# The causal convolution's taps as diagonal matmuls in the opening of a two-layer hybrid kernel

## The chip, the cores and the metric

The kernel runs on one core of a Trainium2 chip. The metric is the time of one execution on the device in microseconds; several runs are taken and their median is used. All times below come from the runs of the kernel before or from one execution of it that the hardware profiler recorded.

## The reference

The input is x of 8 images with 384 channels and 32×32 pixels, in float32. Layer 0 normalises x over the channels and runs a Mamba block over the 1024 pixels in both directions. Layer 1 is causal attention and a feed-forward block with binarized weights and quantized activations, of which only the first five batches need the feed-forward result. What the change touches is this part of layer 0:

```python
xz = jnp.einsum('blc,ec->ble', x, in_proj_w)
u, z = jnp.split(xz, 2, axis=-1)
uc = jax.lax.conv_general_dilated(u.transpose(0, 2, 1), conv1d_w[:, None, :], (1,),
        [(D_CONV - 1, 0)], ..., feature_group_count=C)      # D_CONV = 4
u = silu((uc + conv1d_b[None, :, None]).transpose(0, 2, 1))
x_dbl = jnp.einsum('blc,ec->ble', u, x_proj_w)
dt, Bm, Cm = jnp.split(x_dbl, [dt_rank, dt_rank + D_STATE], axis=-1)
delta = softplus(jnp.einsum('blr,dr->bld', dt, dt_proj_w) + dt_proj_b)
...
h = dA * h + dBu            # the scan over 1024 steps, 16 states
```

The convolution has four taps and one weight per channel and tap. It is done twice, on the sequence and on the reversed one.

## The kernel before, in words

Channels lie on the 128 partitions, so a batch is three chunks (`c`) of 128 channels × 1024 pixels, and each row of 1024 is handled in two halves (`h`) of 512[...]. Every stage is a function that appends steps to a list; lists are interleaved by estimated durations, and a scheduler then fixes the order of the instructions on each engine ahead of time.[...]

`before_scan(b)` makes what the scan of one batch needs. It loads x into a large buffer and normalises it (L324 to L329). For each chunk it then does:

- `in_proj`: three matmuls a half for `u` and for `z` (L336), copied out of PSUM by ACT (L343). The weights `win` are loaded for each chunk.
- `conv(c, d, h)`: one convolution group. In the loop over four taps, the first (s = 0) is an ACT pass that writes the PSUM bank `acc` (L352), the other three are DVE instructions that add weight × shifted `up` to it (L362). ACT adds the bias and writes `u` to SBUF (L363).
- the SiLU on ACT (L423), the sum of both directions (L427), and stores of `u`, `z` and their sum to DRAM.
- `local`: the 3×3 depthwise convolution of the local branch, nine taps, eight of them on DVE (L383), with its gate (L442 to L452).
- `project`: the matmuls xp (L476), summed on DVE in `xd` (L487).

When the three chunks are done, `xd`'s rows for B and C go to DRAM, and `delta` makes 12 tiles of delta and u × delta: a matmul (L507), four ACT passes (L510 to L513), four DVE instructions (L514 to L517) and two stores (L520).

The scan works in units of two states for one half of one chunk in one direction: 96 units a batch. For each, SP loads B and C rows broadcast over the partitions (`bc`), POOL multiplies u × delta by B (`g`, L564), ACT makes the exponential `da` (L577), DVE runs two scans (L582), POOL multiplies by C (L588), and PE transposes and sums in PSUM (L598, eight instructions). POOL's multiplications are kept in program order, and `g` has seven buffers.

**The opening** is what `run(begin)` and `run(first, beside)` make (L1088 to L1096). `begin` is `before_scan` of the first batch. `first` holds the scan units of that batch, and `beside` what goes on beside them: the rest of the first batch's gates, `before_scan` of the second batch, the binarizing of both feed-forward weights (`binarize`, loads at L205 issued from ACT's queue), and `before_scan` of the third and fourth batch. After that come the scans of the other seven batches beside attention (it starts with the output projection, L667) and feed-forward. In that later part `before_scan` of the remaining four batches is laid between feed-forward steps.

Banks of PSUM: two called `s`, two `pt`, two `da`, one `y`, one `av`. In the opening `before_scan` takes turns on `s` and `pt`. In SBUF there are six large buffers of three chunks × 1024 (`btile`), used for x, for weights, for attention and for feed-forward.

Of the kernel before, what the change touches and what calls it, by code (L numbers as in the profile page):

```python
# [12 lines left out]
ALU = mybir.AluOpType  # L13
# [4 lines left out]
P = 128  # L18
B, C, H, W = 8, 384, 32, 32
L = H * W  # L20
NC = C // P
# [5 lines left out]
DCONV = 4  # L27
# [16 lines left out]
ORDER = (0, 1, 2, 3, 5, 6, 4, 7)  # L44
# [3 lines left out]
V_NORM, V_CW, V_CB, V_DTB, V_D, V_DW, V_DWB, V_BP, V_B2, V_ALOG = 0, 1, 5, 6, 7, 8, 17, 18, 19, 20  # L48
# [4 lines left out]
def kernel(  # L53
# [16 lines left out]
    nc = tc.nc  # L70
# [11 lines left out]
    def ctile(name, shape, dt=F32):  # L82
        return const.tile(shape, dt, name=name, tag=name)

    def btile(name):
        return big.tile([P, NC, L], F32, name=name, tag="big")
# [16 lines left out]
    def half(h):  # L103
        return slice(h * HB, (h + 1) * HB)
# [23 lines left out]
    vec = ctile("vec", [P, NC, NV])  # L128
# [8 lines left out]
    for d in range(2):  # L137
        nc.scalar.dma_start(out=wdt[d * DW : d * DW + RANK, :], in_=w_dt)
        nc.scalar.dma_start(
            out=wdt[d * DW + RANK : d * DW + RANK + 1, :],  # L140
# [13 lines left out]
    ident = ctile("ident", [P, P])  # L154
# [147 lines left out]
                    )  # L302


    def before_scan(b, tags, emit, later=None):

        st = {}
        turns = itertools.cycle(tags)
# [1 line left out]
        def bank_of(name):  # L310
            return bank(name, next(turns))
# [33 lines left out]
        def conv(c, d, h):  # L345

            acc = bank_of(f"u{d}_{b}_{c}_{h}")
            up = st["up", c]
            for s in range(DCONV):
                w = vec[:, c, V_CW + DCONV - 1 - s : V_CW + DCONV - s]  # L350
                if s == 0:
                    nc.scalar.activation(acc, up[:, half(h)], AF.Copy, scale=w)  # L352
                    continue
                lo, hi = h * HB, (h + 1) * HB
                if d == 0:
                    t0, t1 = max(lo, s), hi
                    tap = up[:, t0 - s : t1 - s]
                else:
                    t0, t1 = lo, min(hi, L - s)
                    tap = up[:, t0 + s : t1 + s]  # L360
                to = acc[:, t0 - lo : t1 - lo]
                nc.vector.scalar_tensor_tensor(to, tap, w, to, ALU.mult, ALU.add)  # L362
            nc.scalar.activation(  # L363
                st["u", d, c][:, half(h)], acc, AF.Identity, bias=vec[:, c, V_CB : V_CB + 1]
            )

        def local(c, h):

            acc = bank_of(f"loc_{b}_{c}_{h}")
            r0, rows = h * (HB // W), HB // W  # L370
            img = acc.rearrange("p (i j) -> p i j", j=W)
            src = st["xn"][:, c, :].rearrange("p (i j) -> p i j", j=W)
            nc.scalar.activation(  # L373
                acc, st["xn"][:, c, half(h)], AF.Copy, scale=vec[:, c, V_DW + 4 : V_DW + 5]
            )
            for k in range(9):
                di, dj = k // 3 - 1, k % 3 - 1
                if k == 4:
                    continue
                i0, i1 = max(r0, -di), min(r0 + rows, H - di)  # L380
                j0, j1 = max(0, -dj), W - max(0, dj)
                to = img[:, i0 - r0 : i1 - r0, j0:j1]
                nc.vector.scalar_tensor_tensor(  # L383
                    to,
                    src[:, i0 + di : i1 + di, j0 + dj : j1 + dj],
                    vec[:, c, V_DW + k : V_DW + k + 1],
                    to,
                    ALU.mult,
                    ALU.add,
                )  # L390
            return acc

# [10 lines left out]
        for c in range(NC):  # L403
# [13 lines left out]
            for d in range(2):  # L417
                for h in range(NH):
                    emit(lambda c=c, d=d, h=h: conv(c, d, h), 3.0)
# [13 lines left out]
            def gates(c=c, silus=silus, sum_of_us=sum_of_us):  # L433
                st["xc"] = mtile(f"xc_{b}_{c}")
                load(st["xc"], x[b, chunk(c), :])
                accs = [local(c, h) for h in range(NH)]
                with tc.high_priority(offset=60):
                    us = [st["u", 0, c], st["u", 1, c]] if later is None else []
                    silus(us + [st["z", c]])
                    for h in range(NH):  # L440
                        pin(
                            nc.scalar.activation(  # L442
                                accs[h], accs[h], AF.Tanh, scale=0.5, bias=dwbh[:, c : c + 1]
                            )
                        )
                    pin(nc.scalar.preload_act_table_set(LOG_EXP))
                for h in range(NH):
                    acc, xc = accs[h], st["xc"][:, half(h)]
                    nc.vector.scalar_tensor_tensor(
                        acc, acc, 1.0, st["xn"][:, c, half(h)], ALU.add, ALU.mult  # L450
                    )
                    nc.vector.scalar_tensor_tensor(xc, acc, rsh, xc, ALU.mult, ALU.add)  # L452
                spill((b, "t", c), st["xc"], f"st_{b}_{c}")
                spill((b, "z", c), st["z", c], f"sz_{b}_{c}")
                if later is None:
                    sum_of_us()
# [97 lines left out]
    def s_row(u, i):  # L554

        r = sp.tile([P, 2, HB], F32, name=f"bc{i}_{u.name}", tag=f"bc{i}", bufs=(4, 4)[i])
        rows = spilled[u.b, "rows", u.d][i * NS + u.n : i * NS + u.n + 2, half(u.h)]
        load(r, rows.partition_broadcast(P))
        sst["bc", i, u.name] = r
# [497 lines left out]
    def slots(lo, hi):  # L1057
        def at(f, k):
            if 0 <= k < len(units):
                f(units[k])  # L1060

        def slot(k):
            at(s_load, k + AHEAD + 2)
            at(lambda u: s_row(u, 0), k + AHEAD + 2)
            at(lambda u: s_row(u, 1), k + 2)
            at(s_first, k + AHEAD)
            at(s_scan, k)
            at(s_sum, k - 1)
            at(s_gate, k - 1)

        return [(lambda k=k: slot(k), 5.0) for k in range(lo, hi)]

    def run(*lists):
        for f, _ in spread_over(*lists):
            f()

    def steps_of(stage, *args):
        out = Steps()
        stage(*args, out)
        return out  # L1080


# [1 line left out]
    per, ahead = len(units) // B, 3  # L1084
    first = slots(-AHEAD - 2, per + 1)
    others = slots(per + 1, len(units) + 1)
    beside = Steps()
    begin = Steps()  # L1088
    before_scan(ORDER[0], ("s", "pt"), begin, beside)
    run(begin)  # L1090
    beside += steps_of(before_scan, ORDER[1], ("s", "pt"))
    beside += steps_of(binarize, w1, w1s, NC, FF, 2, "w1")
    beside += steps_of(binarize, w2, w2s, NF, C, 8, "w2")
    for b in ORDER[2 : 1 + ahead]:
        beside += steps_of(before_scan, b, ("s", "pt"))
    run(first, beside)  # L1096

    rest, later, due = [], list(ORDER[1 + ahead :]), [(0.0, 0)]
# [74 lines left out]
```

## Time and profile before

| | |
|---|---|
| median of 4 runs | 5245.01 us (5234.74 to 5250.71) |
| the profiled execution | 5253.34 us, span 5251.6 us |
| busy: PE, DVE, ACT, POOL | 4168.3, 3568.1, 2726.4, 3672.5 us |
| share of the span: PE, DVE, ACT, POOL | 79%, 68%, 52%, 70% |
| mean granted TensorE clock | 0.867 |
| HBM traffic | 228 GB/s over the span |

The span is the time between the first and the last instruction of the profiled execution; 1.7 us of its own time lie around it. Busy time is a union: where an instruction overlaps its neighbour on the same engine, the overlap counts once. PE is the matmuls, and PEld their weight loads. The granted clock is the share of full speed at which TensorE ran. Shares over the whole span average over stages with different limits, which is why the profile is also cut into stretches of time.

### The profile page before, as it was taken

How to read it: one execution, taken by the hardware profiler on the slowest of the kernel's cores; microseconds unless marked ns; L12 is line 12 of the kernel's file. 1: busy time of each engine (PE TensorE's matmuls, PEld its weight loads, DVE VectorE, ACT ScalarE, POOL GpSimd, SP SyncE). 2: the span in 40 equal slices, each digit the busy share in tenths (PEclk: the TensorE clock that was granted, in tenths of full speed). 3: DMA queues.
4: the chain of work that ended last, by engine and by line, in shares of the span. 5: the costliest groups of instructions: out<-in, count | busy, mean ns of one | idle time of the engine just before them, and what ended most of it. 6: DMA issues, size and time to landing. Idle time of an engine off the chain costs nothing.

```text
span 5251.6 us, 52624 instructions
## 1 busy us (share of the span) xinstructions
PE 4168.3 (79%) x16458; PEld 2194.2 (42%) x16458; DVE 3568.1 (68%) x4249; ACT 2726.4 (52%) x4914; POOL 3672.5 (70%) x1932
## 2 busy tenths in 40 slices
PE   5465566889787888777897778887888888888899
PEld 2233233444444444434444344443444544444444
DVE  6998887667786657776777766677766665666422
ACT  4665554455653545645556445565355354464434
POOL 0477675977777876759876697867688877887700
PEclk7667676989888899889998889998889899999989
DMA  6778687757678667686676885776966867667500
GB/s 226 272 240 281 229 269 273 246 188 261 208 253 294 209 221 247 207 297 222 234 252 205 270 272 202 237 236 212 305 222 218 275 217 238 212 206 238 190 29 25
DMA packets 625121, 1199.86 MB, mean 228 GB/s; under 512 B 44440, under 2 KB 103240, under 8 KB 624840
## 3 DMA queue, kind: packets, MB, share of 16 engines
q1 hardware_dynamic: 615328, 1180.34, 67.4%
q10 hardware_dynamic: 9512, 16.15, 0.9%
q8 instruction: 130, 2.13, 0.2%
q14 instruction: 151, 1.24, 0.1%
HBM read 1030.65 MB, written 165.68 MB: 228 GB/s over the span
## 4 chain that ended last, share of the span: by engine, by line
POOL 31%; issue 20%; PE 13%; DVE 12%; DMA 7%; ACT 3%; SPq 1%; POOLq 0%; DVEq 0%; ACTq 0%
POOL g L564 17%; POOL g L588 13%; DVE g L582 5%; DMA bc<-rows 5%; PE yp L1000 2%; PE s L753 2%; PE y L598 1%; PE av L839 1%; DVE dp L515 1%; DVE loc L383 1%; PE op L667 1%; DVE u L362 1%; PE pt L825 1%; PE qp L697 1%; POOL carry L587 1%
## 5 line engine op out<-in xcount | busy, mean ns | idle before, releaser
L564 POOL TENSOR_TENSOR g<-ud,bc 128x1024 f32<-128x1024 f32 x768 | 1829.6, 2382 | 832.6 <-PE y L598 414.5
L588 POOL TENSOR_TENSOR g<-g,bc 128x1024 f32<-128x1024 f32 x768 | 1817.7, 2367 | 319.2 <-issue 153.3
L577 ACT ACTIVATE da<-dl,amat 128x512 f32<-128x512 f32 x1536 | 1059.0, 692 | 1634.9 <-DVE g L582 1589.9
L582 DVE TENSOR_TENSOR_SCAN g<-da,g 128x512 f32<-128x512 f32 x768 | 907.0, 1212 | 549.0 <-POOL g L564 512.3
L598 PE MATMUL y<-ident,g 128*128 128x128 f32 x6144 | 962.3, 304 | 371.4 <-POOL g L588 346.5
L582 DVE TENSOR_TENSOR_SCAN g<-da,carry,g 128x512 f32<-128x512 f32 x768 | 956.2, 1273 | 420.5 <-POOL g L564 399.0
L598 PEld LDWEIGHTS y<-ident,g 128*128 128x128 f32 x6144 | 790.0, 157 | 803.0 <-POOL g L588 472.8
L753 PE MATMUL s<-k,q 64*128 64x512 f32 (+3 forms) x1152 | 455.4, 594 | 175.2 <-ACT pr L774 138.5
L773 DVE TENSOR_REDUCE nm<-s 128x1 f32<-128x512 f32 (+3 forms) x576 | 300.7, 546 | 261.1 <-PE s L762 198.2
L774 ACT ACTIVATE pr<-s,nm 128x512 f32<-128x512 f32 (+3 forms) x576 | 329.6, 575 | 151.9 <-DVE nm L773 145.4
L839 PE MATMUL av<-ptn,v 128*64 128x512 f32 (+3 forms) x1152 | 364.4, 543 | 28.6 <-DVE o L851 22.7
L955 PE MATMUL hp<-t,w 128*128 128x512 f32 x720 | 344.7, 624 | 41.5 <-DMA w<-w1s 32.9
L336 PE MATMUL in<-xn,win 128*128 128x512 f32 x576 | 297.1, 660 | 70.1 <-ACT up L343 38.7
L825 PE MATMUL pt<-ident,pr 128*128 128x128 f32 x1728 | 306.6, 300 | 39.6 <-ACT ptn L829 30.9
L1000 PE MATMUL yp<-h,w 128*128 128x512 f32 x720 | 323.6, 608 | 3.4 <-DMA w<-w2s 3.4
L829 ACT COPY ptn<-pt 128x512 f32<-128x512 f32 (+3 forms) x576 | 259.3, 480 | 122.4 <-PE pt L825 120.7
L753 PEld LDWEIGHTS s<-k,q 64*128 64x128 f32 x1152 | 159.2, 203 | 336.1 <-ACT pr L774 216.1
L825 PEld LDWEIGHTS pt<-ident,pr 128*128 128x128 f32 x1728 | 207.2, 151 | 169.3 <-ACT ptn L829 81.8
L697 PE MATMUL qp<-t,wqk 128*128 128x512 f32 x576 | 265.7, 609 | 14.6 <-DVE t L300 14.6
L383 DVE SCALAR_TENSOR_TENSOR loc<-xn,vec,loc 128x496 f32<-128x496 f32 (+3 forms) x384 | 258.5, 730 | 4.0 <-ACT loc L373 3.9
L362 DVE SCALAR_TENSOR_TENSOR u<-up,vec,u 128x512 f32<-128x512 f32 (+3 forms) x288 | 201.4, 747 | 34.5 <-ACT u L352 34.2
L955 PEld LDWEIGHTS hp<-t,w 128*128 128x128 f32 x720 | 136.5, 199 | 199.2 <-issue 152.8
(154 smaller groups left out, 4562.2 us busy)
## 6 DMA issues: line engine op xcount, KB each, us to landing
bc<-rows SPq DMA_DIRECT2D x1536, 512.0 KB, 5.1
t<-st SPq DMA_DIRECT2D x63, 512.0 KB, 6.2
su<-u SPq DMA_DIRECT2D x48, 512.0 KB, 4.3
du<-su SPq DMA_DIRECT2D x96, 256.0 KB, 4.8
sdl<-du SPq DMA_DIRECT2D x96, 256.0 KB, 2.8
sud<-du SPq DMA_DIRECT2D x96, 256.0 KB, 3.4
ud<-sud SPq DMA_DIRECT2D x96, 256.0 KB, 5.6
dl<-sdl SPq DMA_DIRECT2D x96, 256.0 KB, 5.7
```

The lines of the kernel that those rows point to most:

```text
L564: pin(nc.gpsimd.tensor_tensor(g, ud, sst.pop(("bc", 0, u.name)), ALU.mult))
L577: nc.scalar.activation(da, sst["dl", u.b, u.c, u.part], AF.Exp, scale=amat[:, u.c, n : n + 1])
L582: nc.vector.tensor_tensor_scan(gi[:, ::step], da[:, ::step], gi[:, ::step], first, ALU.mult, ALU.add)
L588: pin(nc.gpsimd.tensor_tensor(g, g, sst.pop(("bc", 1, u.name)), ALU.mult))
L598: nc.tensor.matmul(out=y[:, j, :], lhsT=g[:, i, chunk(j)], rhs=ident, is_transpose=True, start=(opens and i == 0 and j == 0), stop=(closes ...
L697: nc.tensor.matmul(out=qp, lhsT=st["wqk"][:, c, o : o + P], rhs=st["xn"][:, c, half(h)], start=(c == 0), stop=(c == NC - 1),)
L753: nc.tensor.matmul(out=ss[e][:, : k1 - k0], lhsT=st["q"][rows_of(e), c, chunk(qi)], rhs=st["k"][rows_of(e), c, k0:k1], start=True, stop=(k ...
L774: nc.scalar.activation(pr, s, AF.Exp, bias=m, accum_out=rs[:, i, e, kb : kb + 1])
L825: nc.tensor.transpose(pt[:, chunk(i)], st["pr", c, g, i, e][:, chunk(j)], ident)
L839: nc.tensor.matmul(out=av[rows_of(e), cols], lhsT=st["v"][:, j, hd * HD : (hd + 1) * HD], rhs=st["ptn", j, e][:, cols], start=(j % QT == 0 ...
L955: nc.tensor.matmul(out=hp, lhsT=st["w1"][:, c, chunk(m % 2)], rhs=st["xn"][:, c, half(h)], start=(c == 0), stop=(c == NC - 1),)
L1000: nc.tensor.matmul(out=yp, lhsT=st["w2", k // 6][:, k % 6, :], rhs=st["h", k // NC][:, k % NC, half(h)], start=(k == 0), stop=(k == NF - 1),)
```

## The change

`before_scan` gets an argument `diags`. Where it is given, all four taps of a convolution group are matmuls whose stationary operand is a 128×128 diagonal matrix with the tap's weights and whose moving operand is the shifted `up`; they are summed in the PSUM bank. The ACT pass that wrote the first tap and the three DVE instructions are gone there. The bias pass on ACT stays. Twelve diagonals (three chunks × four taps) are made on POOL from the identity and the vector of weights, at the place in the program just before the opening. They lie in one large buffer, `taps`. The four `before_scan` of the opening get `diags`; those of the later four batches don't. The change in `local` only names an operand.

```diff
-    def before_scan(b, tags, emit, later=None):
+    def before_scan(b, tags, emit, later=None, diags=None):
...
             for s in range(DCONV):
-                w = vec[:, c, V_CW + DCONV - 1 - s : V_CW + DCONV - s]
-                if s == 0:
+                k = V_CW + DCONV - 1 - s
+                w = vec[:, c, k : k + 1]
+                if s == 0 and diags is None:
                     nc.scalar.activation(acc, up[:, half(h)], AF.Copy, scale=w)
                     continue
...
-                nc.vector.scalar_tensor_tensor(to, tap, w, to, ALU.mult, ALU.add)
+                if diags is None:
+                    nc.vector.scalar_tensor_tensor(to, tap, w, to, ALU.mult, ALU.add)
+                else:
+                    nc.tensor.matmul(
+                        out=to,
+                        lhsT=diags(c, k),
+                        rhs=tap,
+                        start=(s == 0),
+                        stop=(s == DCONV - 1),
+                        skip_group_check=True,
+                    )
...
-    def steps_of(stage, *args):
+    def steps_of(stage, *args, **kwargs):
         out = Steps()
-        stage(*args, out)
+        stage(*args, out, **kwargs)
         return out
...
+    taps = btile("taps").rearrange("p c l -> p (c l)")[:, : NC * DCONV * P]
+    taps = taps.rearrange("p (c k q) -> p c k q", c=NC, k=DCONV)
+    for c in range(NC):
+        for k in range(DCONV):
+            nc.gpsimd.tensor_scalar(
+                taps[:, c, k, :], ident, vec[:, c, V_CW + k : V_CW + k + 1], None, ALU.mult
+            )
+
+    def diags(c, k):
+        return taps[:, c, k - V_CW, :]
+
     beside = Steps()
     begin = Steps()
-    before_scan(ORDER[0], ("s", "pt"), begin, beside)
+    before_scan(ORDER[0], ("s", "pt"), begin, beside, diags)
     run(begin)
-    beside += steps_of(before_scan, ORDER[1], ("s", "pt"))
+    beside += steps_of(before_scan, ORDER[1], ("s", "pt"), diags=diags)
...
     for b in ORDER[2 : 1 + ahead]:
-        beside += steps_of(before_scan, b, ("s", "pt"))
+        beside += steps_of(before_scan, b, ("s", "pt"), diags=diags)
     run(first, beside)
```

More of the change, by code (lines that the diff above doesn't have):

```diff
@@ L382, in local @@
                 to = img[:, i0 - r0 : i1 - r0, j0:j1]
+                tap = src[:, i0 + di : i1 + di, j0 + dj : j1 + dj]
                 nc.vector.scalar_tensor_tensor(
[L384 to L389, printed above, removed]
+                    to, tap, vec[:, c, V_DW + k : V_DW + k + 1], to, ALU.mult, ALU.add
                 )
```

## The prediction

> **What bounds the kernel now.** First the busy time by stage. I cut the span where the trace changes: at 107 us the projections of the first batch are done, at 193 us the scan begins to run steadily, and at 877 us the first output projection (L667) starts, released by the last gated output of batch 0. Columns: stage, its length, then busy us and instruction count of PE, weight loads, DVE, ACT and POOL, then granted clock, DMA share, GB/s.
>
> ```profile
> 0.00:107.00 107.00, 57.12 (x116) 23.42 (x116) 61.76 (x102) 48.31 (x64) 1.34 (x12) 0.79 0.59 205
> 107.00:193.00 86.00, 28.60 (x38) 8.78 (x36) 79.75 (x114) 56.72 (x82) 9.43 (x3) 0.53 0.91 322
> 193.00:877.00 684.00, 404.75 (x1224) 214.46 (x1224) 583.75 (x686) 397.22 (x591) 478.31 (x248) 0.68 0.75 249
> 877.00:5251.00 4374.00, 3677.79 (x15082) 1947.57 (x15082) 2842.87 (x3349) 2224.19 (x4178) 3183.37 (x1669) 0.90 0.67 224
> ```
>
> From 193 to 877 us DVE is busy 583.75/684 = 85% of the time; POOL has 70%, PE 59%, ACT 58%. After 877 us it is PE (84%) and POOL (73%). The change touches only the opening, so it has to pay there; the later 4374 us should start earlier or later by the same amount.
>
> Next, who waits for whom from 193 to 877 us (engine, line, what ended the wait, us in total, times, longest). For DVE:
>
> ```profile
> DVE g L582 <- POOL g L564: 52.7, 26, 4.9
> DVE du L514 <- ACT du L513: 15.3, 7, 4.5
> ...
> DVE u L362 <- ACT u L352: 5.9, 1, 5.9
> ```
>
> for POOL:
>
> ```profile
> POOL carry L587 <- DVE g L582: 86.3, 9, 52.1
> POOL g L564 <- DMA bc<-rows: 69.9, 15, 7.3
> ...
> POOL g L588 <- DMA bc<-rows: 17.3, 7, 9.0
> ```
>
> and for PE:
>
> ```profile
> PE y L598 <- POOL g L588: 193.9, 67, 9.2
> ```
>
> DVE loses about 100 us, half of it to POOL. POOL loses 684 − 478 = 206 us, 87 of them to the broadcast rows; of the 86.3 us put down to the scan, one wait of 52.1 us began at 143 us, before this stage. PE mostly waits for POOL. So DVE sets the pace, with POOL and DMA one step behind. The chain of waits reaches back only to about 690 us, so I don't rest on it.
>
> Last, the groups of the convolution (line engine op, shapes, count | busy, mean ns | idle before), the first row over the whole kernel, the next two from the stretch 193 to 877 us:
>
> ```profile
> L362 DVE SCALAR_TENSOR_TENSOR u<-up,vec,u 128x512 f32<-128x512 f32 (+3 forms) x288 | 201.4, 747 | 34.5 <-ACT u L352 34.2
> ...
> L336 PE MATMUL in<-xn,win 128*128 128x512 f32 x216 | 115.9, 685 | 21.1 <-DVE xc L452 10.8 <-ACT xd L485 8.1 <-DVE xn L329 2.1
> ...
> L352 ACT ACTIVATE u<-up,vec 128x512 f32<-128x512 f32 x36 | 24.3, 683 | 0.0
> ```
>
> A mean includes overlap with the neighbour; what an instruction takes of its engine is busy over count: 201.4/288 = 0.70 us for a tap, 115.9/216 = 0.537 us for a matmul of 512 columns in this stretch.
>
> [...] u times delta (L517, both in SBUF) takes 689 ns up to 130 us, before POOL starts, and 1060 ns from 130 to 860 us, the tap (L362, one operand in PSUM) 751 ns in both. So a removed tap frees its own 0.70 us and no contention. [...] in the trace weight loads of in_proj follow each other every 0.43 us at 36 us, so I take the trace.
>
> **The change, part by part.** 4 batches × 3 chunks × 2 directions × 2 halves = 48 convolution groups lie in the opening: 12 before 107 us, 36 after 193 us.
>
> Removed from DVE: 3 taps a group, 144 in all. The tap groups are 24.8, 24.8 and 24.7 us in 193–400, 400–600 and 600–800 us: 74.3 us. The first batch's 36 taps are 26.2 us. Removed from ACT: the seed L352, 12 × 0.67 + 36 × 0.68 = 32 us; ACT isn't the bound, so that is nothing on the path.
>
> Added to PE: 4 matmuls a group, 192. At 0.537 us the later 144 are 77 us: PE goes from 405 to 482 us of a stage of about 610 us, 79%, under the 84% at which it runs later. The price lies between 0.43 us (full clock) and 0.86 us (the spacing at 29–33 us, where the clock is low): 62 to 124 us; even the upper end leaves PE at 87%. [...] I stay with 0.537.
>
> Added to POOL: 12 diagonal builds, placed after the constants and ahead of every scan instruction. No such row exists; the nearest, a 128x128 select on POOL, takes 0.29 us, so 3.6 us, between 2.5 (the 205 ns memset) and 7. POOL has nothing until 133 us, and the first tap is needed at 37 us, the vectors having landed at 9: nothing on the path. If the build ran late, the first convolution would wait for it.
>
> One of six large buffers is held by the diagonals until the last convolution of the fourth batch (now 775 us). x of four batches and the weights being binarized share the rest; loads L205 are issued from ACT's queue[...]. No such wait shows now. Bounds 0 and 12 us (one load, 12.4 us to landing, come too late); I take 3. No DMA is added or moved and SP's queue keeps its order.
>
> The new wait: a group now needs PE's turn, then one ACT pass, instead of ACT, three DVE turns and ACT. Behind its four matmuls (2.1 us) stand the transposes L598, which free the seven g buffers of POOL; at 59% PE has room. Ahead of them stand transposes that wait for POOL, 193.9/67 = 2.9 us each time. If all of that fell on the path: 36 × 2.9 = 104 us; if the early release of PSUM banks helps, below nothing, some −5. I take 4, since the last convolution is over 100 us before the stage ends.
>
> The start, to 193 us: the taps of chunk 1 run from 62.8 to 72.2 us with binarizing between, PE meanwhile idle for 11 us (to 76.0), after which in_proj of chunk 2 takes 11.2 us instead of 5.3. On PE 16 matmuls at 0.43 are 6.9 us straight after in_proj (ending 64.9), so chunk 1 is hardly earlier[...]; and chunk 2's taps, now 87.8 to 100 us with reductions between, save a little more. I take 8, between 0 and the 26 us removed.
>
> From 193 to 877 us: with DVE's idle time unchanged the stage shrinks by the 74 us removed; with idle in proportion by 74.3/0.85 = 87. I take 74: what waits next is POOL, whose 478 us and 87 us for rows would still fit in 610. DMA at the same traffic goes from 0.75 to 0.75 × 684/610 = 0.84; 107–193 us shows it at 0.91.
>
> Sum: 8 + 74 − 3 − 4 = **75 us**. Against the profiled execution (5253.34, span 5251.6) that is 5178; the median, 5245.01, lies 8 lower: **5170**.
>
> **The rivals.**
> A, the forecast: DVE time comes off nearly whole, 45 to 115 us saved. Chance 0.57.
> B, POOL and DMA take over: the loop POOL, scan, POOL waits for rows as before, and only half of the freed DVE time shortens the stage: 37 us, less a few for the turns: 30 saved, range 11 to 45. For it: 52.7 us of DVE's idle is POOL's, 87 us of POOL's is rows. Against: 70% busy. Chance 0.12.
> C, more than that: the scan's 52.1 us wait at 143–195 us stems from DVE's order and could go with a new one: some 130 saved. Chance 0.05.
> D, slower: PE's turns decide. Transposes that wait for POOL hold back convolutions, and convolutions waiting for `up` hold back transposes, so POOL's g buffers aren't freed. At 2.9 us for each of 36 groups 104 us are added against 82 saved: +22, 5267. It decides from 82/36 = 2.3 us a group. For it: PE's 67 waits, its order fixed in advance. Against: ACT and PE have 40% free. Chance 0.18.
> E, no change: the stage is set by latencies of the scan loop, not by work; or the gain and D cancel. Chance 0.08. That the taps don't reach PE can't be: all four calls pass the diagonals.
>
> **How the numbers follow.** About 0.2%, 10 us, is what a measurement can tell from no change. Faster: A + B + C = 0.74; same: 0.08; slower: 0.18. Range 5128 to 5262: it leaves out C's greater part and the greater part of D, under 0.2 together, and takes in the unknown costs. A's own range is 5130 to 5200.
>
> **What would show it.** Right: no L362 or L352 ahead of the first L667, 192 matmuls at 0.5 us more on PE; DVE busy 100 us less by the first L667, which starts at 877 − 75 = 802 us, give or take 25; PE's clock above 0.68 there; the stretch from L667 to the end 4374 us as before. B shows as longer waits of DVE for L564 and of POOL for rows, with L667 near 847 us. D shows as transposes or tap matmuls waiting longer than 2.3 us a group and L667 after 877 us. A later stretch that changed by over 15 us would break the sum.

## The result, and the profile after

The changed kernel takes **5259.66 us** (median of 44 runs, 5246.45 to 5282.35), the kernel before 5246.53 us beside it (63 runs): ratio 1.003, 95% interval 1.0023 to 1.0038. It is about 13 us slower. The forecast was 5170 us, 75 us faster.

The execution that was profiled took 5249.44 us (span 5247.7, mean granted clock 0.885). First the busy time by stage, cut as before, with the last cut at the first output projection (now L675). Columns: stage, its length, then busy us and count of PE, weight loads, DVE, ACT and POOL, then granted clock, DMA share, GB/s.

```profile
0.00:107.00 107.00, 76.67 (x167) 32.68 (x168) 41.06 (x69) 35.41 (x43) 8.33 (x24) 0.92 0.57 196
107.00:193.00 86.00, 40.59 (x79) 14.88 (x77) 65.01 (x88) 55.33 (x84) 12.72 (x6) 0.65 0.85 289
193.00:890.00 697.00, 483.48 (x1516) 242.85 (x1516) 531.96 (x602) 385.60 (x564) 473.96 (x245) 0.77 0.75 250
890.00:5247.00 4357.00, 3663.53 (x15082) 1947.64 (x15082) 2844.11 (x3349) 2224.61 (x4178) 3182.47 (x1669) 0.91 0.68 225
```

Up to the output projection DVE is busy 638 us (41.06 + 65.01 + 531.96) instead of 725, as meant. Yet the projection starts at 890 instead of 877 us. The stage from 193 us holds 52 us less work for DVE and is 13 us longer; DVE's share fell from 85 to 76%. The last stretch is 17 us shorter here. In the profiles of the other kernels below, none of which changes it, it lies between 4346 and 4374 us, so that is its scatter. The 13 us by which the projection is later agree with the 13 us of the medians.

Then the waits from 193 to 890 us (engine, line, what ended the wait, us in total, times, longest), for DVE:

```profile
DVE g L590 <- POOL g L572: 118.2, 53, 6.6
DVE du L522 <- ACT du L521: 17.0, 10, 4.1
```

for POOL:

```profile
POOL g L572 <- DMA bc<-rows: 119.7, 25, 16.1
POOL carry L595 <- DVE g L590: 35.1, 6, 21.9
...
POOL g L572 <- PE y L606: 14.9, 5, 4.4
```

for PE:

```profile
PE y L606 <- POOL g L596: 91.8, 23, 8.9
PE xp L484 <- ACT u L431: 38.5, 6, 12.9
```

and for the DMA queue of SP:

```profile
SPq L123 <- ACT u L431: 104.4, 12, 14.2
SPq L528 <- DVE du L524: 90.8, 32, 9.6
```

DVE now waits 118 us for POOL's first multiplication (before: 53), and POOL waits 120 us for the rows of B and C (70). A cause of late rows stands in the last view: SP stands for 104 us at the stores of `u`, waiting for the SiLU (L431). In the kernel before, the same wait from 193 to 877 us is 24 us:

```profile
SPq L123 <- ACT u L423: 23.9, 8, 7.9
```

The timeline of SP in the changed kernel shows what that does to the loads behind it (start, us, engine, line, what is issued and how often):

```profile
475.29 7.28 SPq L110 DMA_DIRECT2D bc<-rows  x4
482.62 0.46 SPq L110 DMA_DIRECT2D xc<-in_x  x1
494.56 0.33 SPq L123 DMA_DIRECT2D su<-u  x1
494.99 1.26 SPq L110 DMA_DIRECT2D bc<-rows  x2
```

From 483.1 to 494.6 us SP issues nothing, then the store and, at once, the row loads that stood behind it. So here one waiting store held the loads behind it for 11.5 us.

Why the SiLU is late shows in two views: the groups of the convolution in the first batch, and its first chunk in PE's timeline.

```profile
L367 PE MATMUL u<-up,taps x96: 590/592/593, 46.1 to 122.8; 128*128 128x512 f32 x60, 128*128 128x511 f32 x12, 128*128 128x510 f32 x12, 128*128 128x509 f32 x12
```

```profile
46.07 13.88 PE L367 MATMUL u<-up,taps 128*128 128x512 f32 x32
```

There are 12 groups of four matmuls, 48, in the program, but 96 rows: **one float32 matmul leaves two rows in the profile.** A chunk (four groups, 16 matmuls, 32 rows) takes 13.88 us of PE, 0.43 us a row, so 0.87 us a matmul and 3.5 us a group, at full clock (1.00 from 46 to 60 us) and with nothing in between. On DVE the taps of chunk 0 took 8.8 us (37.7 to 46.5). From the end of the second `up` copy to the end of the first SiLU a chunk of batches 2 to 4 takes 27.9 us on average instead of 18.0, read off the timelines.

### The profile page after: what moved, and what is told of

It reads as the page before. It is cut to its first block, busy times and chain, and to the rows that moved or that the text cites. A ratio compares the mean times of both kernels' runs of the same rounds, so it can differ in the third digit from the quotient of the medians.

```text
span 5247.7 us, 53223 instructions
## 1 busy us (share of the span) xinstructions
PE 4264.3 (81%) x16842; PEld 2238.1 (43%) x16842; DVE 3482.1 (66%) x4105; ACT 2700.9 (51%) x4868; POOL 3677.5 (70%) x1944
## 4 chain that ended last, share of the span: by engine, by line
POOL 32%; issue 22%; DVE 16%; DMA 12%; PE 12%; ACT 5%; SPq 1%; POOLq 0%; ACTq 0%; DVEq 0%
POOL g L572 18%; POOL g L596 13%; DMA bc<-rows 9%; DVE g L590 6%; DVE loc L396 2%; PE s L761 2%; PE yp L1008 2%; DVE dp L523 1%; DVE du L525 1%; PE av L847 1%; DVE u L365 1%; PE in L337 1%; SPq L110 1%; PE qp L705 1%; PE y L606 1%
## 5 line engine op out<-in xcount | busy, mean ns | idle before, releaser
L596 POOL TENSOR_TENSOR g<-g,bc 128x1024 f32<-128x1024 f32 x768 | 1818.7, 2368 | 272.1 <-issue 118.8
L606 PE MATMUL y<-ident,g 128*128 128x128 f32 x6144 | 929.0, 298 | 290.8 <-POOL g L596 268.2
L606 PEld LDWEIGHTS y<-ident,g 128*128 128x128 f32 x6144 | 770.1, 153 | 705.6 <-POOL g L596 376.7
L963 PE MATMUL hp<-t,w 128*128 128x512 f32 x720 | 341.6, 620 | 39.9 <-DMA w<-w1s 27.9
L337 PE MATMUL in<-xn,win 128*128 128x512 f32 x576 | 282.7, 638 | 44.4 <-ACT up L344 36.6
L1008 PEld LDWEIGHTS yp<-h,w 128*128 128x128 f32 x720 | 137.7, 194 | 172.6 <-issue 170.3
```

Of the source, the lines that this page charges most:

```text
L337: nc.tensor.matmul(out=mp, lhsT=st["win", c][:, k, i, :], rhs=st["xn"][:, k, half(h)], start=(k == 0), stop=(k == NC - 1),)
L596: pin(nc.gpsimd.tensor_tensor(g, g, sst.pop(("bc", 1, u.name)), ALU.mult))
L606: nc.tensor.matmul(out=y[:, j, :], lhsT=g[:, i, chunk(j)], rhs=ident, is_transpose=True, start=(opens and i == 0 and j == 0), stop=(closes ...
L963: nc.tensor.matmul(out=hp, lhsT=st["w1"][:, c, chunk(m % 2)], rhs=st["xn"][:, c, half(h)], start=(c == 0), stop=(c == NC - 1),)
L1008: nc.tensor.matmul(out=yp, lhsT=st["w2", k // 6][:, k % 6, :], rhs=st["h", k // NC][:, k % NC, half(h)], start=(k == 0), stop=(k == NF - 1),)
```

## The experiments

**How the tables are read.** "Starts" is the start of the first delta matmul (the projections of batch 0 are done), "op" the start of the first output projection; "blocks" is the sum of the lengths of the three blocks in which batches 2 to 4 get their deltas (first delta matmul to last u × delta), "between" that of the stretches from the end of one block to the start of the next, in which the projections and convolutions lie. "Rows in a block" counts the loads of B and C rows that the fixed order of SP has between a block's first and last store of u × delta, for batches 2, 3, 4. The last column is SP's wait for `u` between "starts" and "op". "No taps" leaves out DVE's three taps; ACT's pass with the first tap stays. Ratios are to the kernel before on the same chip; 0.001 is 5.2 us.

| | ratio, 95% | starts | op | blocks | between | rows in a block | SP for u |
|---|---|---|---|---|---|---|---|
| before | 1 | 107.3 | 877.8 | 236 | 476 | 12, 11, 10 | 24 |
| after | 1.0030 (1.0023–1.0038) | 130.7 | 890.4 | 226 | 488 | 13, 14, 10 | 104 |
| e1 no taps | 0.9950 (0.9932–0.9968) | 90.9 | 846.6 | 244 | 458 | 11, 11, 10 | 17 |
| e2 first batch only | 1.0030 (1.0017–1.0044) | 129.8 | 887.8 | 241 | 472 | 12, 11, 10 | 24 |
| e3 later batches only | 1.0003 (0.9992–1.0014) | 118.8 | 879.3 | 226 | 490 | 13, 14, 10 | 105 |
| e4 after, u on ACT | 0.9905 (0.9879–0.9930) | 130.0 | 829.7 | 175 | 485 | 6, 7, 5 | 0 |
| e5 before, u on ACT | 0.9992 (0.9979–1.0004) | 107.7 | 864.1 | 225 | 477 | 12, 10, 10 | 0 |
| e6 bf16 taps | 0.9967 (0.9954–0.9979) | 101.9 | 857.1 | 243 | 446 | 10, 11, 10 | 52 |
| e7 bf16, u on ACT | 0.9967 (0.9954–0.9981) | 102.2 | 862.9 | 237 | 467 | 11, 11, 10 | 0 |
| e8 late taps | 0.9893 (0.9876–0.9911) | 106.0 | 833.1 | 173 | 488 | 7, 7, 5 | 0 |
| e9 late taps, z too | 0.9925 (0.9905–0.9946) | 107.7 | 836.8 | 164 | 502 | 4, 6, 4 | 0 |
| e10 late taps, bf16 | 0.9982 (0.9970–0.9995) | 105.5 | 866.7 | 234 | 460 | 13, 11, 10 | 0 |
| e11 no taps, u on ACT | 0.9964 (0.9947–0.9980) | 92.5 | 852.5 | 240 | 457 | 13, 10, 10 | 0 |
| e12 after, fewer units | 1.0015 (1.0001–1.0029) | 133.1 | 875.9 | 211 | 493 | 10, 8, 6 | 91 |
| e13 before, fewer units | 0.9987 (0.9970–1.0003) | 106.1 | 865.3 | 225 | 484 | 9, 8, 5 | 36 |
| e14 no taps, fewer units | 0.9928 (0.9907–0.9949) | 90.8 | 826.8 | 233 | 457 | 8, 8, 6 | 11 |
| e15 after, u on ACT, more units | 0.9947 (0.9934–0.9959) | 132.8 | 849.8 | 215 | 463 | 11, 12, 9 | 0 |
| e16 before, u on ACT, fewer units | 0.9948 (0.9935–0.9961) | 107.8 | 842.3 | 185 | 496 | 5, 6, 5 | 0 |
| e17 no taps, u on ACT, fewer units | 0.9936 (0.9915–0.9957) | 93.4 | 837.4 | 217 | 469 | 8, 6, 6 | 0 |

### What the taps were worth: e1

```diff
                 if s == 0:
                     nc.scalar.activation(acc, up[:, half(h)], AF.Copy, scale=w)
+                    continue
+                if bare:
                     continue
```

In the opening the loop ends after the first tap: ACT's pass stays, DVE's three taps are left out, and nothing is put on PE.

> The kernel before, with the three DVE taps of each convolution group left out in the opening (the convolution there keeps only its first tap, so u is another one); nothing is put on TensorE. Theory Q (the opening is set by the fixed order of the queues: SP's row loads wait behind stores of the projections, and the chain of a chunk counts by its latency): freeing 100 us of DVE brings little, the first output projection starts at 845 to 865 us instead of 877.8, most of it from the start. Theory D (my forecast: DVE's load sets the pace, and the gain was eaten by TensorE's price): the first output projection starts near 795 us and the time falls by about 80 us.

With DVE's taps gone and nothing in their place, 26 us came off in all (0.995). From the first delta matmul to op the opening went from 770 to 756 us: 15 us, where the forecast took 74 for that part alone. So the main step had failed before PE entered: DVE's time does not come off at its own size. The waits of e1 show where it goes. From 193 to 847 us, for POOL, then DVE:

```profile
POOL g L566 <- DMA bc<-rows: 90.3, 21, 7.9
```

```profile
DVE g L584 <- POOL g L566: 91.4, 43, 8.2
```

The freed DVE stands waiting for POOL (before: 53 us), and POOL for rows (70), though SP waits only 17 us for `u` here. So late rows have more causes than that wait.

### First batch or later batches: e2 and e3

Only the first `before_scan` gets `diags` (e2), or only the other three (e3); the diagonals are built at the same place in both.

```diff
-    before_scan(ORDER[0], ("s", "pt"), begin, beside, diags)
+    before_scan(ORDER[0], ("s", "pt"), begin, beside)
```

> Diagonal taps for the first batch alone. Both theories: the start, where nothing else runs, loses its 23 us (first delta matmul at 131 us instead of 107). Theory Q: the stage after it takes as long as before (770 us), so the first output projection starts near 901 us, and the time is some 23 us over the kernel before. If the stages trade with one another (the scan catches up), it starts nearer 885.

> Diagonal taps for the second to fourth batch, the first batch on DVE. Additive: start as before (107 us), then 760 us as in the changed kernel, first output projection near 867 us, time 10 us under the kernel before. Theory D, if TensorE's price cancels: no better than 877. Theory Q allows either, but waits for rows stay near 120 us, as in the changed kernel, and not near 70.

e2 has the late start (129.8 us), reaches op 10 us later than before and not 23, and has a ratio of 1.003; e3's is 1 within the interval (10 us less were expected if the parts add), though SP's wait for `u` is 105 us and the projection stretches are as long as in the changed kernel (490 us). e3 still starts at 118.8 us with the first batch's taps on DVE. That is half of the late start, and comes from where the build stands, as e8 below starts at 106.0. A part of it shows in the trace: in the changed kernel the first load of x is issued at 3.93 us instead of 0.74, and DVE's fixed order has the sums over the weight load ahead of the normalisation of x (first and last line: DVE's reduction and normalisation, after; between them PE's sums).

```profile
27.86 1.48 DVE L223 TENSOR_REDUCE sums_w<-w 128x1 f32<-128x614 f32 x2
...
29.40 0.59 PE L226 MATMUL mps_w<-sums_w,ones_w 128*128 128x5 f32 x2 [6.92 <-DVE sums_w L223]
...
33.35 4.04 DVE L330 SCALAR_TENSOR_TENSOR xn<-xn,vec,ms 128x512 f32<-128x512 f32 x6
```

With the build moved behind the first batch (e8) that normalisation starts at 26.82 us, before the change at 27.39, in the changed kernel at 33.35: 6 of the 12 us. So with SP's queue as it was, the first batch's taps cost 14 us (after against e3; with the build 16, e2 against before), and the later batches', from which most of the gain was to come, bring 0 (e3 against before, after against e2). Within the intervals the whole loss is thus the first batch's, and it comes without a longer wait of SP for `u` (24 us in e2); e3 has the longer wait and no loss. The next runs ask why the later batches bring nothing.

### SP's queue: e4 and e5

The stores of `u` in the opening are issued from ACT's queue instead of SP's, in the changed kernel (e4, whose line is shown) and in the kernel before (e5).

```diff
-                    spill((b, "u", d, c), st["u", d, c], f"su_{d}_{b}_{c}")
+                    spill((b, "u", d, c), st["u", d, c], f"su_{d}_{b}_{c}", nc.scalar if diags else None)
```

> The changed kernel, with the 24 stores of u in the opening issued from ACT's queue (ACT makes u itself) instead of SP's, where they waited 104.6 us for ACT with the row loads behind them. Theory Q: SP's waits for u vanish, POOL's waits for rows fall from 120 to 70 us or less, and the first output projection starts 30 to 60 us earlier than in the changed kernel (830 to 860 us). Theory D: rows are not what sets the pace, it starts within 5 us of 890.

> The kernel before (all taps on DVE) with the opening's stores of u issued from ACT's queue. In it those stores wait 24 us on SP, against 104.6 in the changed kernel. Theory Q: the queue alone is worth those 24 us at most, the first output projection starts at 855 to 875 us and the time falls by 5 to 20 us; the 60 us of the former run need both, the freed DVE and the freed queue. Rival R: the queue alone does it, it starts near 820 us (60 earlier), and taps on TensorE are worth nothing or less.

e4 gains 66 us on the changed kernel (1.003 to 0.9905) and starts as late as it; e5 gains nothing measurable, where 5 to 20 us were expected. Of SP's 104 us about 45 only move: its waits at the stores of `z` and of the sum of `u` grow from 26 and 21 to 54 and 38 us. And 51 of e4's 61 us at op lie in the delta blocks, where no `u` is stored, and there the fixed order has only 6, 7 and 5 row loads instead of 13, 14 and 10. The edit had changed the order too, since that is made from the whole program. e15 to e17 take the two apart.

### A shorter matmul: e6, e7 and e10

`up` and the diagonals are bfloat16 (e6); with the `u` stores on ACT's queue as well (e7); and that with the late build of e8 (e10).

```diff
-                st["up", c] = mtile(f"up_{b}_{c}")
+                if diags:
+                    st["up", c] = mid.tile([P, L], BF16, name=f"up_{b}_{c}", tag="mid")
...
```

> The changed kernel with diagonals and `up` in bf16 (in the opening alone; u is a little less exact): a group is then four rows on TensorE instead of eight, each at most as long. Theory Q in its form 'TensorE's long groups make u late': the chunks of the first batch come 6 to 10 us earlier each (first delta matmul at 100 to 112 us instead of 131), SP's waits for u in the stage fall from 105 to about 60 us, the first output projection starts at 845 to 870 us. If the length of a group doesn't matter in the stage, only the start moves and it starts near 870 with the stage still 760 us long.

> The changed kernel with bf16 diagonals and `up` in the opening (u a little less exact) and the stores of u on ACT's queue. If the two repairs (short groups, free queue) act on different waits, they add: 33 and 61 us off 890, first output projection near 800 us. If both act on the same one, SP's wait for u, the second brings little: 820 to 835 us.

> First batch on DVE, diagonals built late and in bf16 (as `up` of batches two to four), stores of u on ACT's queue. Against the fp32 form of the same, first output projection 833 us: the same within 10 us if the length of a group no longer matters once SP is free, 15 to 35 us earlier if it does.

In e6 a chunk's 16 tap matmuls take 3.62 us, a quarter, and one row each:

```profile
47.46 3.62 PE L367 MATMUL u<-up,taps 128*128 128x512 bf16 x16
```

The time from copy to SiLU falls to 18.9 us, SP's wait for `u` to 52 us, and the kernel to 0.9967: 33 us better than with float32 taps. That points to the length of the group as what makes the change slower, but it isn't alone in the edit: PE has less work in all, and the order has 10, 11, 10 row loads instead of 13, 14, 10. Freeing the queue then brings no more (e7), and a late build nothing either (e10). Both miss their expectations: op at 863 instead of 800 or 820 to 835 us (e7), and 34 us later than e8 instead of level or earlier (e10). That is also less than e15 below would let one expect of e7; a possible cause, the granted clock, stands at the end.

### A late build: e8 and e9

The diagonals are built after `run(begin)`, the first batch keeps its taps on DVE, and the `u` stores are on ACT's queue; in e9 the stores of `z` too.

```diff
     run(begin)
+    taps = ...
```

> The first batch on DVE as before, the diagonals built in the program after the first batch's steps instead of ahead of them, batches two to four with diagonal taps, and the opening's stores of u from ACT's queue. Theory Q (the start lost 23 us, half by the new order that the early build brings, half by longer groups; the stage gains 60 when SP is freed): first delta matmul at 105 to 112 us, stage about 700 us, first output projection at 805 to 820 us, time 60 to 75 us under the kernel before. If the build's place has no part in it, the first delta matmul comes at 119 us as in the run with diagonals from the second batch on.

> The kernel of the run before this one, with the opening's stores of z (also made by ACT) issued from ACT's queue as well. Theory Q: SP's waits for z, 58 us in the kernel with u's stores moved, leave its queue, and the stage gets shorter by another 5 to 25 us. Rival: what is left is POOL's and DVE's own loop, no change within 5 us.

e8 starts 24 us earlier than e4 and reaches op at 833 us (expected: 805 to 820), e4 at 830; the ratios 0.9893 and 0.9905 are equal within their intervals. **With the `u` stores off SP's queue, a start that is earlier by 24 us brings nothing at the end**; the cost of the first batch's taps that e2 showed is gone there too. e8 has the lowest median of the study, 5182.93 us (five runs). e9 takes more from SP's queue and gains nothing, against both of its expectations; it is some 17 us slower, with intervals that just touch. Its projection stretches grow by 14 us, and SP now waits 63 us for the sums of `u` (34 in e8).

### No taps, queue free: e11

> The DVE taps of the opening left out (u is another one) and nothing on TensorE, as in the first run, with the opening's stores of u on ACT's queue. It closes the table of taps (on DVE, left out, on TensorE) by queue (SP, ACT). Theory Q: with the queue freed, freed DVE time pays at last: against the run with taps on DVE and u on ACT's queue (first output projection at 864 us) it starts 50 to 80 us earlier, and it bounds what taps on TensorE can reach (829.7). Rival: without taps it is no earlier than 845, so the 60 us of the changed kernel with u on ACT's queue are luck of an order.

The edits of e1 and e5 together. Nothing is gained over e1: without taps SP waits only 17 us for `u`, so there is little to free. Op at 852.5 us is where the expectation's rival put it, "no earlier than 845": e4's 61 us at op weren't the free queue alone. e15 shows that the order made 20 of them.

### The order alone: e12, e13 and e14

Each delta weighs 1.8 instead of 3.0 where the lists of the opening are interleaved, so fewer scan units, with their row loads, come to lie among the deltas; in after (e12), before (e13) and e1 (e14).

```diff
-                emit(lambda c=c, d=d, h=h: delta(c, d, h), 3.0)
+                emit(lambda c=c, d=d, h=h: delta(c, d, h), 1.8 if len(tags) == 2 else 3.0)
```

> The changed kernel, u's stores on SP, with the same weight of 1.8 for a delta step of the opening. Row loads in the blocks of SP's order: 10, 8, 6 instead of 13, 14, 10. Theory O: the blocks shrink from 72, 78 and 75 us towards the 55 to 61 of the run with u's stores on ACT's queue, the stretches between them stay, as DVE is free there, and the first output projection starts at 830 to 860 us instead of 890. Theory Q: still within 10 us of 890, as SP's wait of 105 us for u stays.

> The kernel before, all taps on DVE, with one number changed: a delta step of the opening is weighted 1.8 instead of 3.0 when steps and scan units are interleaved, so fewer units lie among the deltas (row loads between a block's first and last delta store in SP's order: 9, 8, 5 instead of 12, 11, 10). Theory O (order: the three delta blocks, 76 to 81 us each, are as long as they are because units lie in them): blocks of 58 to 66 us, first output projection 15 to 45 us before 877.8. Theory Q (freed SP queue made the 60 us): no change beyond 10 us, as u's stores stay on SP. If DVE has no room for the units among the projections, those stretches grow by what the blocks lose.

> Taps of the opening left out (u is another one), nothing on TensorE, and the weight of 1.8. Row loads in the blocks 8, 8, 6. Theory O with a part for DVE: freed DVE time pays once units lie where it is free, so against the same without taps left out it gains 20 to 60 us in the stage; first output projection 790 to 820 us. If DVE's taps aren't on the pace even then, it gains no more than the 15 us that leaving them out brought at a weight of 3.0.

All three are lower, by 7 to 12 us in the ratio (each about as wide as its interval) and by 12 to 20 us at op, less than expected: the order counts, but doesn't make e4's short blocks by itself.

### Queue and order crossed: e15, e16 and e17

e15 is e4 with a weight of 5.0 (order as long as in after), e16 is e5 with 1.5, e17 is e11 with 1.8.

> The changed kernel with the u stores on ACT's queue (the kernel of the 829.7 us opening), but each delta weighs 5.0 instead of 3.0 in the interleaving, so that 11, 12 and 9 row loads stand between the stores of a delta block instead of 6, 7 and 5. If a free SP queue and a short order are both needed for the short delta blocks: the blocks grow back from 175 us to about 220 to 240, the first output projection starts at 870 to 890 us, the time is 0.998 to 1.003. If the order does not matter here: blocks 175 to 185, output projection about 830, time about 0.99.

> The kernel before (taps on ACT and DVE), u stores on ACT's queue, and each delta weighs 1.5, so that 5, 6 and 5 row loads stand in a delta block. If a free queue and a short order together make the short blocks, whatever engine has the taps: blocks 170 to 190 us instead of 225, output projection 815 to 835 us, time 0.987 to 0.992, as the kernels with taps on TensorE reached. If TensorE's taps are needed for it: blocks 215 to 225, output projection 855 to 865, time about 0.998.

> No taps in the opening at all (the convolution's four taps are left out there, so that u is the bias alone before SiLU), u stores on ACT's queue, each delta weighs 1.8 (8, 6 and 6 row loads in a delta block). If queue and order together set the blocks: 175 to 200 us instead of 240, output projection 790 to 815 us, time 0.985 to 0.990; against the kernel before with both (previous run) this is then what removing the taps is worth once the order no longer hides it, 15 to 30 us. If something else holds the blocks: 230 to 240, output projection about 830 to 850, time 0.993 to 0.996.

In e15 the blocks grow from 175 to 215 us with the weight as the only edit, and op and ratio lie between its two expectations. The first block of e4, then of e15, in the columns of the first view:

```profile
355.00:411.00 56.00, 34.56 (x88) 15.58 (x88) 55.83 (x66) 40.13 (x69) 25.86 (x13) 0.60 0.73 238
```

```profile
355.00:424.00 69.00, 35.79 (x105) 19.00 (x105) 64.87 (x72) 43.83 (x76) 36.99 (x17) 0.58 0.66 223
```

DVE is at 99.7% in e4's block, with 11 multiplications of POOL inside instead of 15 (and two short copies in each). Half of what a short block saves comes back between the blocks (463 to 485 us), where the units went; 20 us remain at op. e16 has short blocks without TensorE's taps (185 us, in the range of the first theory), but op at 842 and a ratio of 0.9948, short of both that it named. e17 has blocks between its two expectations, but op and ratio where "something else holds the blocks" put them, and gains 6 us on e16 instead of 15 to 30. Its edit, like e1's, leaves ACT's pass with the first tap in; the expectation's "no taps at all" is not what was run. The ratios by taps, queue and order:

| taps | SP, long | SP, short | ACT, long | ACT, short |
|---|---|---|---|---|
| DVE | 1 | 0.9987 | 0.9992 | 0.9948 |
| TensorE, float32 | 1.0030 | 1.0015 | 0.9947 | 0.9905 |
| none on DVE, first on ACT | 0.9950 | 0.9928 | 0.9964 | 0.9936 |

- **Queue.** With the order roughly alike, moving the `u` stores is worth 44 and 58 us with TensorE's taps, 4 and 20 with DVE's, and nothing measurable (7 and 4 us slower) without taps. That is the ranking of SP's waits for `u`: 91 to 104, 24 to 36, 11 to 17 us.
- **Order.** The short one is worth 7 to 23 us in every row. The numbers of row loads in a "short" or "long" order differ by up to 5 from kernel to kernel, so these are sizes, not exact terms.
- **The change.** With the queue free it gains 24 and 23 us, as the forecast's sign; with the stores in SP's queue it loses 16 and 15. So where the `u` stores stand turns the sign. e2 and e3 add that this has two parts: with the stores on SP the later batches gain nothing, and the first batch costs 14 us.

That the rows then come in time is seen in e15's waits (193 to 840 us, for POOL, then DVE), where POOL's 103.2 and DVE's 116.6 us of the changed kernel in the same stretch have become

```profile
POOL g L572 <- DMA bc<-rows: 39.2, 14, 8.3
```

```profile
DVE g L590 <- POOL g L572: 79.9, 36, 5.5
```

## Why the prediction was wrong, point by point

- **Removed from DVE and ACT: right as work.** DVE has 87 us less up to op, of 100.5 forecast; no tap is left on it there. Half of the difference is the sums of both directions: nine of them take 18.2 us of the stage, 2.03 us each, before 11.0, 1.23 us each; why they got longer was not shown.
- **"With DVE's idle time unchanged the stage shrinks by the 74 us removed": the step that failed first.** Removing DVE's taps outright gives 26 or 31 us over the whole kernel with SP's queue as it was, 15 or 6 with the queue free (last table). 85% busy was not the pace: DVE waited for POOL and POOL for rows, which were listed as "one step behind". Rival B named this, and its signs came (DVE's and POOL's waits above); its price, half of the freed time, 37 us, was still too high for the stage (15 us in e1). The first ground of rival E, that latencies of the scan loop set the stage, fits e1 best.
- **PE, 0.537 us a matmul: mis-sized.** The 216 rows of in_proj that I divided by are 108 matmuls. In the stage the taps took 129.6 us for 144 matmuls, 0.90 us each, outside my upper bound of 0.86:

```profile
L367 PE MATMUL u<-up,taps 128*128 128x512 f32 (+3 forms) x288 | 129.6, 602 | 0.4 <-ACT u L375 0.4
```

  The spacing of 0.43 us that I read off the trace is one row's, and a float32 matmul is two rows: 0.87 us at full clock. PE's sum came out right all the same (483 us against 482), by luck: the taps took 52 us more than priced, while the clock rose from 0.68 to 0.77 and the rest of PE's work took about 50 us less, the transposes alone 124 us instead of 159. What mattered was the latency of a group: 3.5 us against 2.1.
- **"SP's queue keeps its order", PE's turn 4 us: the step that lost what gain was left.** No DMA was added, but a `u` store that waits for a later SiLU held the row loads behind it (11.5 us at 483 us, above). I followed who waits behind PE's matmuls as far as the transposes and `g` buffers and didn't ask what is queued behind the store. POOL waits only 14.9 us for the transposes; SP's wait rose by 81 us. Taking it away moved the kernel by 44 to 58 us. It is not the loss itself, which e2 has without that wait.
- **Rival D** was right in sign and nearly in its condition: a chunk takes 9.9 us longer, 2.5 us a group, above the 2.3 from which it was to decide. Its path was wrong. With the same groups on PE and the stores elsewhere (e15), the change gains; PE's waits for POOL even fell from 194 to 92 us.
- **The start, 8 us saved: wrong**, the first delta is 23 us later: half from the build's place (e3), half from the longer groups. It costs 14 to 16 us with SP's queue as it was (e2), which is about the size of the whole loss, and nothing measurable with the stores elsewhere (e4 against e8). Most of the 8 was my estimate for chunk 2's in_proj, from a misread line: 5.3 us is only the half of chunk 1's in_proj that lies after 60 us, 12 rows of 24. The whole takes 10.63 us, so chunk 2's 11.15 is hardly longer:

```profile
54.31 10.63 PE L336 MATMUL in<-xn,win 128*128 128x512 f32 x24
```

- **POOL's build, 3.6 us: 7.0 measured**, the upper bound; not waited for, but its place in the program moved the fixed order, which I had not costed:

```profile
2.81 7.00 POOL L1100 TENSOR_SCALAR taps<-ident,vec 128x128 f32<-128x128 f32 x12 [0.92 <-DMA vec<-in_vecs]
```

- **The big buffer, 3 us**: an estimate; no run takes it alone, so it stays untested. **The later stretch**: changed by 17 us in the profile, within its scatter among kernels.

**What stays open.** Why an outright removal of DVE's taps with queue and order both free brings only 6 us (e16 to e17), and why bfloat16 taps with a free queue (e7) don't beat e15. A rival that no run separates is the granted clock. From the first delta matmul to op it is 0.75 in the changed kernel and 0.78 in e4, which have float32 taps in the later batches, and 0.67, 0.67, 0.65 and 0.66 in the kernel before, e5, e11 and e17, which have none on PE; in e7, with bfloat16 taps, it is 0.69 from 102 to 848 us. Where it was higher the transposes took less of PE: from 193 us to op, in e15 (0.80), then in e7:

```profile
L606 PE MATMUL y<-ident,g 128*128 128x128 f32 x779 | 121.8, 313 | 85.5 <-POOL g L596 83.9 <-ACT yt L617 1.5
```

```profile
L609 PE MATMUL y<-ident,g 128*128 128x128 f32 x784 | 146.5, 349 | 151.1 <-POOL g L599 143.0 <-ACT yt L620 8.0
```

So some of what e4, e8 and e15 gain may come with the higher clock, and not from the work taken off DVE; that is an estimate from these numbers. Besides, the runs without taps keep ACT's first pass (48 of 0.68 us), which the change removes.

In all runs with a free queue op lies at 850 to 867 us with a long order and 830 to 842 with a short one, almost whatever is done with the taps and the start. That points to the loop of row loads, POOL and scan as the limit there; which link of it was not isolated, since none of the runs varies the row loads themselves. Nor do they show why a late start costs something only with the `u` stores in SP's queue.

## What to carry to other kernels

Before work is moved to an engine with room, compare the latency of the moved step (here 3.5 us a group, priced at 2.1), not only the sum of its work, and follow its consumer to the end: one store that waited for it held the row loads behind it for 11.5 us, and moving such stores to another queue was worth 44 to 58 us with the taps on TensorE. A busy share of 85% was no bound here, as the engine's remaining waits ended on another loop; the cheap test is to leave the work out and see what comes off (15 us of the stage, where 74 were forecast). Where the order of instructions is made from the whole program, an edit at one place can move work at another (in e4 from 13, 14 and 10 row loads in a block to 6, 7 and 5), so cross the edit with the order before a gain is put down to either.

## What the runs showed of the hardware

In the changed kernel a float32 matmul of 512 columns appears as two rows, 0.43 us apart at full clock, 0.87 us in all (13.88 us for 16, clock 1.00 from 46 to 60 us); the same in bfloat16 is one row and 0.23 us (e6, 3.62 us for 16). A 128x128 product of a tile with a value per partition took POOL 0.58 us (12 in 7.00 us, at 2.81 us).
